# Two graph-attention layers on one core: the order of the last four turns and of a few opening steps is changed

## The chip, the cores and the metric

The kernel runs on one core of a Trainium2 chip. A core has a matrix engine (TensorE, PE in the profile; its weight loads are listed as PEld), VectorE (DVE), ScalarE (ACT), GpSimd (POOL) and SyncE (SP), which here issues all DMAs. Each engine works through its own queue of instructions in order; semaphores tie the engines together. TensorE writes its results to eight banks of PSUM, from which VectorE and ScalarE read them.

The metric is the device time of one execution in microseconds (us). Before the change the median of three runs is 2775.55 us (2774.35 to 2775.74).

## What is computed

Two layers of attention over 128 graphs of 128 nodes with 512 features, in float32. Cut to what matters:

```python
# layer 0: 4 heads of 64, mask adj;  layer 1: 8 heads of 64, mask adj or the diagonal
q, k, v = split_heads(h @ Wq), split_heads(h @ Wk), split_heads(h @ Wv)
sim  = einsum('bhid,bhjd->bhij', q, k) * 64 ** -0.5
attn = softmax(where(mask, sim, very_negative))
out  = merge_heads(einsum('bhij,bhjd->bhid', attn, v)) @ Wo + bo
x    = layernorm(x + out)      # after each of the two layers
# layer 0: h = x;  layer 1: h = layernorm(x) * gamma + beta, Wq, Wk, Wv from w_qkv
```

## The kernel before, in words

The 128 graphs are taken in 64 groups of two. The kernel is a pipeline written out by hand: the schedule is manual, so the order of the calls in the source is the order in which each engine gets its instructions. A turn `step(s)` works on five groups at once: the projections of layer 0 for group s, scores and softmax of layer 0 for group s-1, attention and output product of layer 0 for group s-2, the projections of layer 1 (`qk`, `v`) for group s-3, the scores and softmax of layer 1 for group s-4, and attention and output product of layer 1 for group s-5. `opening()` does the first groups and turns the weights of layer 1, `step(s)` runs for s = 2 to 63, and then `closing_a()` (turn 64), `closing_b(65)`, `closing_b(66)` and `last()` (turn 67) empty the pipeline. Each of these closings has its own order of calls.

Three parts of work come in every turn: part 0 is the softmax of layer 0 (both graphs), parts 1 and 2 are those of layer 1, one for each graph. For each part `masked` copies the scores under the mask into a cleared tile `sm` (VectorE), `maxima` takes the negative maxima (VectorE), `exps` takes the exponentials and their sums (ScalarE, four per half), `normalised` takes the reciprocal of the sums (VectorE) and multiplies (GpSimd), `blocks` transposes 32 by 32 blocks (VectorE) and writes them to DRAM, `probs_arrive` fetches them in transposed order into `pT`, and `attend` multiplies them with v (TensorE) and copies the result to `aT` (ScalarE). `blocks_direct` transposes on TensorE instead. `cleared` sets the next `sm` tiles (GpSimd).

The products with weights use a scheme of seven half-size products in place of eight (Winograd's form of Strassen's). They are numbered 1 to 7 and accumulate in three banks:

```python
    INTO = {1: ("a", True), 2: ("c", True), 6: ("a", False), 5: ("f", True), 7: ("a", False),
            4: ("a", False), 3: ("f", False)}
```

Bank a takes 1, then 6, 7 and 4 on top of it; bank f takes 5, then 3. Between two products of one bank the partial sum must be read out: a later product waits for that read. In `qk` and `v` ScalarE copies the partial sums of 1, 5 and 6 away (`tap`, tiles `ev` and `eqk`, L348), VectorE adds them to 2, 7 and 3, and ScalarE copies 4. In `out_product` VectorE adds each of the seven to the residual row block `r` (L502). The sums of inputs (`sums`, `out_sums`, L303) are made on GpSimd, and the sums of weights (`weight_sums`, `combine`, L186) once at the beginning, on VectorE and GpSimd; those of layer 1's q and k, second block, are made in turn 3, one subtraction at a time between other work.

`stats` takes mean and variance of the finished rows (VectorE), `roots` takes the reciprocal root (GpSimd, L699 to L714) and puts two things off into lists: `norms` (ScalarE normalises the rows, and for layer 1 a DMA writes them out) and, for layer 0, `ratios` (GpSimd). `flush()` issues what is in the first list, `flush(latest)` the second. `addend` scales the rows by the ratio (ScalarE, L679) and adds the bias (GpSimd, L680).

Tiles with one tag share one buffer: a new tile waits until the one before has been read. `AT[0, g]` (tile `aT` of layer 0) lies in tag `qo1`, and `SO[0, g]` (its sums) in `qo0`, the buffers of layer 1's q, which `qk` products 7 and 3 write.

`last()` ends with `out_plain`, the output product of the last group without the scheme, in banks a0 and f0, and `norm_plain`, its addition and norm.

Of the kernel before, what the change touches and what calls it, by code (L numbers as in the profile page):

```python
# [17 lines left out]
P = 128  # L18
D = 64
G = 2  # L20
# [7 lines left out]
def kernel(ctx: ExitStack, tc: tile.TileContext, x, adj, wq, wk, wv, wo, bo,  # L28
# [28 lines left out]
    def flush(what=later):  # L57
        while what:
            what.pop(0)()
# [110 lines left out]
    wsqk = const.tile([P, 3, KH, I1], F32, name="wsqk")  # L170
    wsv = const.tile([P, 3, KH, I1 // 2], F32, name="wsv")

    def weight_sums(w, ws, *blocks_, steps=range(4)):

        for c in blocks_:
            h0, h1 = (1, 0) if w is w1qk else (0, 1)
            b11, b12 = w[:, c, h0], w[:, c, h1]
            b21, b22 = w[:, KH + c, h0], w[:, KH + c, h1]
            combine(b11, b12, b21, b22, ws[:, 0, c], ws[:, 1, c], ws[:, 2, c],
                    eng=nc.gpsimd if w is w1qk and c == 0 else nc.vector, steps=steps)  # L180

    def combine(b11, b12, b21, b22, t2, t3, t4, eng=nc.vector, steps=range(4)):

        todo = ((b12, b12, b11), (t2, b22, b12), (t3, t2, b11), (t4, b21, t2))
        for o, a, b in (todo[i] for i in steps):
            eng.tensor_tensor(o, a, b, op=ALU.subtract)  # L186

    def weight_sums_0():
# [352 lines left out]
    def with_self(g):  # L541

        if 0 <= g < NG:
            nc.vector.tensor_tensor(M[g], M[g], eye[:, None, :].to_broadcast([P, G, N]), op=ALU.max)
# [91 lines left out]
    def attend(s, *parts):  # L636

        for part in parts or PARTS:
            l = min(part, 1)
            g = s - (2, 5)[l]  # L640
            if not 0 <= g < NG:
                continue
            K = (K0, K1)[l]
            if part != 2:
                AT[l, g] = one.tile([P, G, K, N], F32, tag=("qo1", "aT1")[l], name=f"aT{l}_{g}")
            pT = PT.pop((g, part))
            if part == 2:
                pm = mm_tile(f"av{part}_{g}")
            else:
                pm = ps_st.tile([P, 512], F32, tag="af"[part], name=f"av{part}_{g}")  # L650
            pm = pm.rearrange("p (k n) -> p k n", n=N)

            for b in range(G) if l == 0 else (part - 1,):
                for h in range(HEADS[l]):
                    i, kk = h % 2, h // 2
                    at = b * K0 + kk if l == 0 else kk
                    v = (qkv0[:, b, kk, 0 if g % 2 else 3, i * D:(i + 1) * D] if l == 0
                         else V[1, g][:, b, h * D:(h + 1) * D])
                    nc.tensor.matmul(pm[i * D:(i + 1) * D, at, :].rearrange("p (a r) -> p a r", r=32), v,  # L659
                                     pT[:, :, i * K1 + at, :], start=True, stop=True)  # L660
            if l == 0:
                nc.scalar.copy(AT[l, g].rearrange("p b k n -> p (b k) n"), pm)
            else:
                nc.scalar.copy(AT[l, g][:, part - 1], pm)  # L664

    def out_sums(l, g):
        if not 0 <= g < NG:
            return
        K = HEADS[l] // 2
        so = SO[l, g] = one.tile([P, 4, K // 2, N], F32, tag=("qo0", "xs0")[l], name=f"so{l}_{g}")  # L670
        halves_sums(so, AT[l, g].rearrange("p b (h c) n -> p b h c n", h=2))

    def addend(l, g):
# [96 lines left out]
    def v(g, *which):  # L770
        for i in which:
            product("v", g, i)

    def qk(g, *which):
        for i in which:
            product("qk", g, i)
# [43 lines left out]
    def step(s):  # L820
# [22 lines left out]
        out_product(0, s - 2, 1, 2, *(() if s == 2 else (5,)))  # L843
        maxima(s, 2)
        product_0(s, 2)
        normalised(s, 0)
        out_product(0, s - 2, *((5,) if s == 2 else ()), 6, 3)
        exps(s, 1, 0)
        stats(0, s - 2, 0)
        if s == 2:  # L850
            turn(0, s + 1)
            arrive(0, s + 1)
        if s == 3:
            weight_sums(w1qk, wsqk, 1, steps=(0,))
        product_0(s, 6)
        exps(s, 1, 1)
        out_product(0, s - 2, 7)
        (blocks_direct if s == 2 else blocks)(s, 0)
        if s == 3:
            weight_sums(w1qk, wsqk, 1, steps=(1,))  # L860
        product_0(s, 5)
        out_product(0, s - 2, 4)
        normalised(s, 1)
        finish(s - 3, 0)
        stats(0, s - 2, 1)
        if s == 3:
            weight_sums(w1qk, wsqk, 1, steps=(2,))
        exps(s, 2, 0)
        product_0(s, 7)
        finish(s - 3, 1)  # L870
# [1 line left out]
        blocks(s, 1)  # L872
        product_0(s, 3)
        if s == 3:
            weight_sums(w1qk, wsqk, 1, steps=(3,))
        if s > 2:
            turn(0, s + 1)
        product_0(s, 4)
# [41 lines left out]
        out_product(1, s - 5, 7, 3, 4)  # L920
        q_in_order(s - 3)
        addend(0, s - 1)
        v(s - 3, 7)
        stats(1, s - 5, 0)
        v(s - 3, 3)
        stats(1, s - 5, 1)
        v(s - 3, 4)
        if s > 2:
# [4 lines left out]
    def closing_a():  # L933

        s = NG
        made = scores(s, 1, 2)
        attend(s, 0)
        masked(made, s, 1, 2)
        out_sums(0, s - 2)
        finish(s - 3, 0)  # L940
        attend(s, 1, 2)
        made = scores(s, 0)
        maxima(s, 1)
        out_product(0, s - 2, 1, 2)
        masked(made, s, 0)
        finish(s - 3, 1)
        out_product(0, s - 2, 5, 6)
        maxima(s, 2)
        flush()
        load_rows(s - 1)  # L950
        exps(s, 1, 0)
        qk(s - 3, 1)
        out_product(0, s - 2, 7, 3, 4)
        qk(s - 3, 2)
        stats(0, s - 2, 0)
        stats(0, s - 2, 1)
        maxima(s, 0)
        exps(s, 1, 1)
        qk(s - 3, 6)
        addend(1, s - 5)  # L960
        out_sums(1, s - 5)
        exps(s, 2, 0)
        qk(s - 3, 5)
        normalised(s, 1)
        out_product(1, s - 5, 1, 2)
        flush()
        exps(s, 2, 1)
        qk(s - 3, 7)
        blocks(s, 1)
        out_product(1, s - 5, 5, 6)  # L970
        normalised(s, 2)
        flush(latest)
        exps(s, 0, 0)
        qk(s - 3, 3)
        blocks(s, 2)
        probs_arrive(s, 1, 2)
        out_product(1, s - 5, 7, 3)
        exps(s, 0, 1)
        normalised(s, 0)
        out_product(1, s - 5, 4)  # L980
        qk(s - 3, 4)
        cleared(s + 1, 1, 2)
        addend(0, s - 1)
        addend(1, s - 4)
        stats(1, s - 5, 0)
        stats(1, s - 5, 1)
        with_self(s - 2)

    def closing_b(s):

        only = s == NG + 1
        made = scores(s, 1, 2)
        masked(made, s, 1, 2)
        v(s - 4, 1, 2)
        maxima(s, 1)
        exps(s, 1, 0)
        v(s - 4, 6, 5)
        if only:
            blocks(s - 1, 0)
            probs_arrive(s - 1, 0)  # L1000
        maxima(s, 2)
        flush()
        v(s - 4, 7, 3, 4)
        exps(s, 1, 1)
        attend(s, 1, 2)
        out_sums(1, s - 5)
        finish_direct(s - 3)
        exps(s, 2, 0)
        out_product(1, s - 5, 1, 2)
        normalised(s, 1)  # L1010
        attend(s, 0)
        out_sums(0, s - 2)
        qk(s - 3, 1)
        out_product(1, s - 5, 5, 6)
        exps(s, 2, 1)
        qk(s - 3, 2)
        blocks(s, 1)
        out_product(1, s - 5, 7, 3)
        normalised(s, 2)
        qk(s - 3, 6)  # L1020
        out_product(1, s - 5, 4)
        out_product(0, s - 2, 1, 2)
        qk(s - 3, 5)
        blocks(s, 2)
        probs_arrive(s, 1, 2)
        out_product(0, s - 2, 5, 6)
        stats(1, s - 5, 0)
        stats(1, s - 5, 1)
        out_product(0, s - 2, 7, 3, 4)
        qk(s - 3, 7)  # L1030
        stats(0, s - 2, 0)
        stats(0, s - 2, 1)
        cleared(s + 1, 1, 2)
        flush()
        qk(s - 3, 3, 4)
        flush(latest)
        addend(1, s - 4)
        with_self(s - 2)

    def last():  # L1040

        s = NG + 3
        made = scores(s)
        masked(made, s, 1)
        maxima(s, 1)
        v(s - 4, 1)
        attend(s)
        exps(s, 1, 0)
        masked(made, s, 2)
        maxima(s, 2)  # L1050
        exps(s, 1, 1)
        out_product(1, s - 5, 1, 2)
        exps(s, 2, 0, 1)
        out_sums(1, s - 5)
        normalised(s, 1)
        v(s - 4, 2, 6)
        addend(1, s - 4)
        v(s - 4, 5)
        out_product(1, s - 5, 6, 5)
        whole_again()  # L1060
        normalised(s, 2)
        v(s - 4, 7)
        blocks_direct(s, 1)
        v(s - 4, 3)
        out_product(1, s - 5, 7, 3)
        stats(1, s - 5, 0)
        out_product(1, s - 5, 4)
        v(s - 4, 4)
        attend(s + 1, 1)
        stats(1, s - 5, 1)  # L1070
        blocks_direct(s, 2)
        flush()
        out_plain(NG - 1, 0, 0)
        attend(s + 1, 2)
        out_plain(NG - 1, 0, 1)
        norm_plain(NG - 1, 0)
        out_plain(NG - 1, 1, 0, 1)
        norm_plain(NG - 1, 1)

    opening()  # L1080
# [35 lines left out]
```

## Time and profile before

| | |
|---|---|
| median of three runs | 2775.55 us |
| the profiled execution's own time | 2776.21 us |
| its span, first to last instruction | 2774.4 us |
| TensorE matmuls busy | 2744.8 us, 99% of the span |
| TensorE weight loads busy | 2180.9 us |
| VectorE busy | 1945.2 us |
| ScalarE busy | 1526.4 us |
| GpSimd busy | 1748.5 us |
| DMA, mean over the span | 202 GB/s |
| mean granted TensorE clock | 0.998 |

The busy share of TensorE in 40 equal slices of the span is nine tenths or more in all but the first and the last two. Turn 2 begins at about 37 us of the span, turn 3 at 56.5, turn 4 at 93, turn 64 (`closing_a`) at 2628.5, turn 65 at 2663.8, turn 66 at 2703.4 and turn 67 (`last`) at 2737.1; the last matmul ends at 2767.9.

A row of a timeline gives the start, the duration of one merged group, engine, line, operation, output tile and input tile, and in brackets the idle time before it and the engine and line that ended it.

### The profile page before, as it was taken

To read this page: it belongs to the slowest core of one execution; us is meant where nothing else is said; L and a number is where in the kernel's file an instruction comes from. 1 tells how busy PE (TensorE), PEld (TensorE's weight loads), DVE (VectorE), ACT (ScalarE), POOL (GpSimd) and SP (SyncE) were. 2 spreads that over 40 slices of the span, in tenths; PEclk is the share of its full clock that TensorE was granted. 3 is DMA by queue.
4 is the path that set the end of the run, shared out by engine and by line. 5 is a ranking of instruction groups with operands and counts; after the bars stand their busy time and mean duration, and the time that the engine had idled before them with its cause. 6 is when DMAs were issued, how large, how long until landed. Compare 5 with 4: busy or idle time off the path is not lost.

```text
span 2774.4 us, 53786 instructions
## 1 busy us (share of the span) xinstructions
PE 2744.8 (99%) x18353; PEld 2180.9 (79%) x18353; DVE 1945.2 (70%) x3537; ACT 1526.4 (55%) x4869; POOL 1748.5 (63%) x2311
## 2 busy tenths in 40 slices
PE   8999999999999999999999999999999999999988
PEld 8978778778777787787787777877877877878777
DVE  5677677677677776776776776777767767767654
ACT  4456465465565564554655655645546556556454
POOL 5566666666666666666666666666666666666654
PEclk9999999999999999999999999999999999999999
DMA  5567877777777778778777777787787777777731
GB/s 170 154 197 206 223 209 210 216 209 215 211 209 221 207 208 222 208 208 220 210 212 214 208 220 209 210 220 208 206 223 208 210 215 209 217 210 210 190 107 54
DMA packets 473760, 561.42 MB, mean 202 GB/s; under 512 B 52104, under 2 KB 366992, under 8 KB 473488
## 3 DMA queue, kind: packets, MB, share of 16 engines
q1 hardware_dynamic: 473488, 557.99, 71.7%
q8 instruction: 147, 2.41, 0.4%
q14 instruction: 125, 1.02, 0.1%
HBM read 299.37 MB, written 258.47 MB: 201 GB/s over the span
## 4 chain that ended last, share of the span: by engine, by line
PE 96%; DVE 1%; ACT 1%; POOL 1%; issue 0%; DMA 0%; SPq 0%; POOLq 0%; ACTq 0%; DVEq 0%
PE qka L339 16%; PE a L460 13%; PE oa L498 12%; PE va L339 8%; PE qkf L339 8%; PE av L659 6%; PE f L460 6%; PE of L498 6%; PE qkc L339 4%; PE vf L339 4%; PE c L460 3%; PE oc L498 3%; PE sc L531 2%; PE sc L536 2%; PE vc L339 2%; PE sc_a L536 2%
## 5 line engine op out<-in xcount | busy, mean ns | idle before, releaser
L580 ACT ACTIVATE sm<-sm,nmax 128x128 f32<-128x128 f32 x1536 | 595.8, 395 | 9.3 <-DVE nmax L571 5.5
L589 POOL TENSOR_TENSOR sm<-sm,rec 128x1024 f32<-128x1024 f32 x192 | 364.1, 1896 | 274.9 <-DVE rec L588 274.9
L680 POOL TENSOR_TENSOR r<-r,bias 128x1024 f32<-128x1024 f32 x128 | 301.6, 2356 | 142.0 <-ACT r L679 142.0
L502 DVE TENSOR_TENSOR r<-oa,r 128x256 f32<-128x256 f32 x508 | 212.1, 417 | 173.5 <-PE oa L498 139.2
L580 ACT ACTIVATION_READ_ACCUMULATOR sm<-sm,nmax 128x1 f32 x1536 | 298.2, 194 | 0.0
L348 ACT COPY ev<-va 128x256 f32<-128x256 f32 x128 | 47.6, 372 | 433.7 <-PE va L339 433.7
L699 POOL TENSOR_SCALAR ve<-mv 128x2 f32<-128x2 f32 x191 | 41.6, 218 | 377.8 <-DVE mv L692 367.3
L607 DVE STREAM_TRANSPOSE turnedp<-sm 128x1024 f32<-128x1024 f32 x188 | 233.5, 1242 | 45.7 <-POOL sm L589 40.5
L303 POOL TENSOR_TENSOR xs<-xT 128x256 f32<-128x256 f32 x256 | 187.1, 731 | 112.4 <-ACT xT L257 91.6
L571 DVE TENSOR_REDUCE nmax<-sm 128x8 f32<-128x1024 f32 x192 | 226.2, 1204 | 0.1
L339 PE MATMUL qka<-wsqk,xs 128*128 128x512 f32 x472 | 221.8, 592 | 0.0
L339 PE MATMUL qkf<-w,xs 128*128 128x512 f32 x472 | 221.8, 592 | 0.0
L498 PE MATMUL oa<-wso,so 128*128 128x256 f32 x760 | 206.2, 380 | 3.3 <-DVE rec L588 2.4
L498 PE MATMUL of<-wo,so 128*128 128x256 f32 x760 | 206.7, 381 | 1.5 <-DVE r L502 1.4
L725 ACT ACTIVATE r<-r,shift,root 128x512 f32<-128x512 f32 x254 | 192.7, 807 | 10.6 <-POOL shift L714 10.6
L565 DVE COPY_PREDICATED sm<-m,sc 128x512 f32<-128x512 uint8 x256 | 172.9, 728 | 13.0 <-PE sc L531 3.1
L339 PEld LDWEIGHTS qkf<-w,xs 128*128 128x128 f32 x472 | 89.7, 190 | 112.9 <-issue 112.9
L339 PEld LDWEIGHTS qka<-wsqk,xs 128*128 128x128 f32 x472 | 89.7, 190 | 112.9 <-issue 98.8
L691 DVE BATCH_NORM_STATS2 st<-r 128x6 f32<-128x512 f32 x254 | 174.9, 689 | 2.3
L551 POOL MEMSET sm<- 128x1024 f32 x192 | 174.9, 952 | 0.0
L303 POOL TENSOR_TENSOR so<-aT 128x256 f32<-128x256 f32 (+1 forms) x254 | 150.5, 592 | 23.5 <-ACT aT L664 20.1
L498 PEld LDWEIGHTS of<-wo,so 128*128 128x128 f32 x760 | 143.7, 190 | 22.4 <-issue 2.5
(182 smaller groups left out, 6788.8 us busy)
## 6 DMA issues: line engine op xcount, KB each, us to landing
scrp<-turnedp SPq DMA_DIRECT2D x188, 512.0 KB, 3.2
pT<-scrp SPq DMA_DIRECT2D x252, 256.0 KB, 4.7
scr<-turned SPq DMA_DIRECT2D x123, 512.0 KB, 3.0
raw<-scr SPq DMA_DIRECT2D x492, 128.0 KB, 3.9
r<-in_x_dram SPq DMA_DIRECT2D x63, 512.0 KB, 3.7
out_dram<-r SPq DMA_DIRECT2D x63, 512.0 KB, 3.4
pT<-scrp SPq DMA_DIRECT2D x248, 128.0 KB, 4.1
x<-in_x_dram SPq DMA_DIRECT2D x61, 512.0 KB, 5.9
```

The source lines that it names most:

```text
L303: nc.gpsimd.tensor_tensor(o, a0, a1, op=op)
L339: nc.tensor.matmul(o, lhsT, rhs, start=first and m == 0, stop=m == len(todo) - 1, skip_group_check=True)
L460: nc.tensor.matmul(acc[:, at * P:(at + 1) * P], lhsT, rhs, start=first and n == 0, stop=n == len(todo) - 1, skip_group_check=True)
L498: nc.tensor.matmul(acc, left[:, c], right[:, c], start=first and c == 0, stop=c == hk - 1, skip_group_check=True)
L502: nc.vector.tensor_add(part, acc, part)
L551: nc.gpsimd.memset(sm, NEG1 if part else NEG0)
L571: nc.vector.tensor_reduce(NMAX[part], SM[part], AX.X, ALU.max, negate=True)
L580: nc.scalar.activation(sm[:, i, k, :], sm[:, i, k, :], AF.Exp, bias=nmax[:, i, k:k + 1], accum_out=total[:, i, k:k + 1])
L589: nc.gpsimd.tensor_tensor(SM[part], SM[part], rec[:, :, :, None].to_broadcast([P, 2, K1, N]), op=ALU.mult)
L607: nc.vector.transpose(t.rearrange("p q (h r) -> p q h r", r=32), SM.pop(part).rearrange("p i k (q r) -> p q (i k) r", r=32))
L680: nc.gpsimd.tensor_tensor(R[g], R[g], (bias0, bias1)[l][:, None, :].to_broadcast([P, G, E]), op=ALU.add)
L725: nc.scalar.activation(R[g][:, b], R[g][:, b], AF.Identity, bias=shift[:, b:b + 1], scale=root[:, b:b + 1])
```

## The change

It moves calls in turns 2 to 4 and in the four closings, and gives two tiles of the last group (63) other buffers. No arithmetic is added or removed.

- Turn 2: the output products 5 and 6 are called before `normalised(s, 0)`.
- Turn 3: the four subtractions of `weight_sums(w1qk, wsqk, 1)` stand together, behind `product_0` 3; the argument `steps` goes.
- Turns 3 and 4: product 3 of v stands before product 7.
- Group 63: `AT[0, 63]` in tag `x`, `SO[0, 63]` in tag `raw0`.
- `closing_a`: VectorE's transposes of parts 1 and 2 and the reciprocal of part 2 stand behind additions of the output product; `addend(1, 60)` before `addend(0, 63)`; part 0 is transposed and fetched at the end of this turn, not within the next.
- `closing_b`: v's copies of products 6 and 5 stand before all exponentials; part 1 is normalised and transposed before the attention's sums; exponentials of part 2 after the attention of part 0; output products of layer 0 lie between the products of qk; `norms` at the end stand behind the key copy (qk 4) and `addend`; in turn 66 `addend(1, 63)` is called too.
- `last`: the attention before v's other products, v's copies between the exponentials, `out_plain` in one piece per graph.

```diff
@@ step
         product_0(s, 2)
+        if s == 2:
+            out_product(0, s - 2, 5, 6)
         normalised(s, 0)
-        out_product(0, s - 2, *((5,) if s == 2 else ()), 6, 3)
+        out_product(0, s - 2, *(() if s == 2 else (6,)), 3)
...
-        if s == 3:
-            weight_sums(w1qk, wsqk, 1, steps=(0,))
...
-            weight_sums(w1qk, wsqk, 1, steps=(3,))
+            weight_sums(w1qk, wsqk, 1)
...
-        v(s - 3, 7)
+        v(s - 3, 3 if s < 5 else 7)
         stats(1, s - 5, 0)
-        v(s - 3, 3)
+        v(s - 3, 7 if s < 5 else 3)
@@ attend, out_sums
-tag=("qo1", "aT1")[l]
+tag=("qo1", "aT1", "x")[2 if (l, g) == (0, NG - 1) else l]
-tag=("qo0", "xs0")[l]
+tag=("qo0", "xs0", "raw0")[2 if (l, g) == (0, NG - 1) else l]
@@ closing_a
         qk(s - 3, 7)
+        out_product(1, s - 5, 5, 6)
         blocks(s, 1)
-        out_product(1, s - 5, 5, 6)
+        exps(s, 0, 0)
+        qk(s - 3, 3)
+        out_product(1, s - 5, 7, 3)
         normalised(s, 2)
         flush(latest)
-        exps(s, 0, 0)
-        qk(s - 3, 3)
+        exps(s, 0, 1)
+        out_product(1, s - 5, 4)
         blocks(s, 2)
         probs_arrive(s, 1, 2)
-        out_product(1, s - 5, 7, 3)
-        exps(s, 0, 1)
+        qk(s - 3, 4)
         normalised(s, 0)
-        out_product(1, s - 5, 4)
-        qk(s - 3, 4)
         cleared(s + 1, 1, 2)
+        addend(1, s - 4)
         addend(0, s - 1)
-        addend(1, s - 4)
         stats(1, s - 5, 0)
         stats(1, s - 5, 1)
         with_self(s - 2)
+        blocks(s, 0)
+        probs_arrive(s, 0)
@@ closing_b
         v(s - 4, 1, 2)
         maxima(s, 1)
+        v(s - 4, 6, 5)
         exps(s, 1, 0)
-        v(s - 4, 6, 5)
-        if only:
-            blocks(s - 1, 0)
-            probs_arrive(s - 1, 0)
         maxima(s, 2)
-        flush()
-        v(s - 4, 7, 3, 4)
+        v(s - 4, 7, 3)
         exps(s, 1, 1)
+        v(s - 4, 4)
+        normalised(s, 1)
         attend(s, 1, 2)
         out_sums(1, s - 5)
+        blocks(s, 1)
         finish_direct(s - 3)
-        exps(s, 2, 0)
         out_product(1, s - 5, 1, 2)
-        normalised(s, 1)
         attend(s, 0)
         out_sums(0, s - 2)
+        exps(s, 2, 0)
         qk(s - 3, 1)
+        flush()
...
-        blocks(s, 1)
         out_product(1, s - 5, 7, 3)
-        normalised(s, 2)
         qk(s - 3, 6)
         out_product(1, s - 5, 4)
-        out_product(0, s - 2, 1, 2)
+        normalised(s, 2)
         qk(s - 3, 5)
+        out_product(0, s - 2, 1, 2, 5)
         blocks(s, 2)
         probs_arrive(s, 1, 2)
-        out_product(0, s - 2, 5, 6)
+        qk(s - 3, 7)
+        out_product(0, s - 2, 6, 3)
         stats(1, s - 5, 0)
+        out_product(0, s - 2, 7)
         stats(1, s - 5, 1)
-        out_product(0, s - 2, 7, 3, 4)
-        qk(s - 3, 7)
+        qk(s - 3, 3)
+        out_product(0, s - 2, 4)
+        cleared(s + 1, 1, 2)
+        qk(s - 3, 4)
+        addend(1, s - 4)
+        if s == NG + 2:
+            addend(1, s - 3)
         stats(0, s - 2, 0)
         stats(0, s - 2, 1)
-        cleared(s + 1, 1, 2)
         flush()
-        qk(s - 3, 3, 4)
         flush(latest)
-        addend(1, s - 4)
@@ last
         v(s - 4, 1)
-        attend(s)
         exps(s, 1, 0)
         masked(made, s, 2)
+        attend(s)
+        out_sums(1, s - 5)
+        v(s - 4, 2, 6)
         maxima(s, 2)
+        v(s - 4, 5)
         exps(s, 1, 1)
         out_product(1, s - 5, 1, 2)
...
         out_product(1, s - 5, 4)
...
+        out_plain(NG - 1, 0, 0, 1)
         stats(1, s - 5, 1)
-        blocks_direct(s, 2)
         flush()
-        out_plain(NG - 1, 0, 0)
-        attend(s + 1, 2)
-        out_plain(NG - 1, 0, 1)
+        out_plain(NG - 1, 1, 0, 1)
         norm_plain(NG - 1, 0)
-        out_plain(NG - 1, 1, 0, 1)
         norm_plain(NG - 1, 1)
```

## What I predicted, and why

> **What bounds the kernel now.** I read first the table of busy time by stretch, then TensorE's waits in the closing, then the timelines of the engines that end them. The chain that ended last is 96% TensorE, and in the middle TensorE does not idle at all:
>
> ```profile
> 0.00:160.00 160.00, 151.40 (x1214) 135.85 (x1215) 100.68 (x179) 77.00 (x237) 87.58 (x119) 1.00 0.53 162
> 160.00:2600.00 2440.00, 2440.00 (x16060) 1915.62 (x16059) 1750.38 (x3173) 1369.18 (x4378) 1568.24 (x2072) 1.00 0.76 212
> 2600.00:2774.40 174.40, 153.37 (x1083) 129.41 (x1081) 94.11 (x186) 80.24 (x255) 92.62 (x120) 0.97 0.36 100
> ```
>
> (Stretch, length, busy us of TensorE matmul, weight load, VectorE, ScalarE, GpSimd, granted clock, DMA share, GB/s.) Matmuls are neither added nor removed, and from turn 5 to the last full turn no engine's order changes. So only idle time can move: 8.6 us in the opening, 21.0 us in the closing, 6.5 us of that after the last matmul. The waits in the closing are:
>
> ```profile
> PE va L339 <- ACT ev L348: 4.8, 3, 2.0
> PE oa L498 <- DVE r L502: 3.0, 5, 0.9
> PE oa L498 <- DVE rec L588: 2.4, 1, 2.4
> PE av L659 <- DMA pT<-scrp: 2.1, 1, 2.1
> PE sc L536 <- ACT kt L432: 1.5, 1, 1.5
> PE qka L339 <- ACT aT L662: 0.7, 1, 0.7
> ```
>
> One loss is in no list of waits. After the 2.38 us wait the clock was granted at half:
>
> ```profile
> 2654.00:2655.00 1.00, 0.00 (x0) 1.00 0.00 0
> 2657.00:2658.00 1.00, 1.00 (x3) 0.50 0.28 93
> 2662.00:2663.00 1.00, 1.00 (x7) 0.50 0.17 27
> 2664.00:2665.00 1.00, 1.00 (x20) 1.00 1.00 238
> ```
>
> Finer stretches put the half clock at 2656.44 to 2663.27. Product 3 (of), product 4 (oa) and qka then took 1.75, 2.07 and 3.13 us, against 1.03, 1.03 and 1.95 elsewhere: about 2.9 us lost.
>
> [...] the two drops, at 2656.44 and, after the last matmul, 2772.47, lie 116.03 us apart, 34 windows of 3.413 us. [...] 2.29 us of idle inside one window dropped it, 1.8 us (at 2711.0 to 2712.8) didn't; and a window with 0.88 us idle kept it at half. [...]
>
> **The opening** (one answer each). Turn 2: the reciprocal at 44.81 waited for exponentials with the addition of product 5 behind it, and product 3 waited 1.43 us. With the additions first product 3 waits about 0.3, but the normalisation still ends at 46.99, so the transposes after it wait some 0.5: gain 0.65. Turn 3: the weight sums (0.6 to 0.8 us each) between additions cost waits of 0.53 and 0.67; after the additions they are done by about 74.2, and product 6 of qk needs them at 75.6 or later: gain 1.2. Turns 3 and 4: product 3 of v between 6 and 7 hides the 0.46 us wait for a copy, but product 4 must then wait for the addition of product 7 (matmuls 1.03, addition 0.42, where product 3 had lain): 0. Sum 1.85.
>
> **The closing, replayed by hand** with the durations of before; times on its clock, the opening's gain kept apart.
>
> Closing a, turn 64. Products 5 and 6 of the output are added before the transpose of part 1, so product 7 starts at 2652.8, not 2655.3. The transpose still waits for GpSimd until 2653.3 (1.2 us), then the addition for qo (0.6); product 7 is added by 2655.45, and product 4, ready at 2654.6, starts at 2655.5. One wait of 0.9 replaces 2.38 and 0.88, and the half clock goes: the next scores start at 2658.35, not 2663.83. Gain 5.5.
>
> Turn 65, start. The normalisation of part 0 can't be earlier (2659.36 as before: its reciprocal stands behind part 2's transpose). Then come on VectorE the statistics, the moved transpose of part 0 (2661.3 to 2662.5), four masked copies (2.5), one addition (0.35), two maxima (1.13 each), and only then, at 2668.0, product 7 of v is added. The copies of partial sums are early now, so products 7 and 3 don't wait; product 4, ready at 2665.6, waits 2.4 until 2668.05. Before, it started at 2673.37. Gain 5.3: the 2.0 us wait for the copy became this one.
>
> Turn 65, rest. ScalarE copies aT before exponentials, but attention must end first: the 0.7 us stays. The waits of 0.52, 0.61 and 0.73 for additions of the two output products nearly go (about 0.3 left), since qk's products now lie between them, which the tags x and raw0 permit. The scores of turn 66 start at 2696.15, not 2703.42. Gain 7.25.
>
> Turn 66, start. These rows tell what stands in the way:
>
> ```profile
> 2704.00 1.52 ACT L725 ACTIVATE r<-r,shift,root 128x512 f32<-128x512 f32 x2 [3.73 <-POOL shift L714]
> 2705.42 0.56 ACT L432 COPY kt<-qka 128x512 f32<-128x512 f32 x1
> 2705.89 1.33 ACT L679 ACTIVATE r<-r,ratio 128x512 f32<-128x512 f32 x2
> ...
> 2702.41 0.19 POOL L699 TENSOR_SCALAR ve<-mv 128x2 f32<-128x2 f32 x1 [3.69 <-DVE mv L692]
> ...
> 2707.30 2.36 POOL L680 TENSOR_TENSOR r<-r,bias 128x1024 f32<-128x1024 f32 x1
> ```
>
> The key copy kt now leads on ScalarE, so the scores don't wait 1.46. But on GpSimd the bias addition of group 61 now stands before the roots of group 63, and on ScalarE the norm of 63 stands before v's copies. From the end of product 4 at 2696.25: kt and ratios 1.85, bias 2.4, roots 1.6, norm 1.4, copy 0.4: product 6 of v starts at 2703.9, though ready at 2700.1. A new wait of 3.75 takes what kt and the later 1.98 us copy wait give: gain 5.0 at product 6; 7.05 at product 7, which no longer waits.
>
> Turn 66, end, and last. Rows of before:
>
> ```profile
> 2728.38 0.18 DVE L588 RECIPROCAL rec<-total 128x8 f32<-128x8 f32 x1
> 2730.05 0.42 DVE L502 TENSOR_TENSOR r<-oa,r 128x256 f32<-128x256 f32 x1 [1.49 <-PE oa L498]
> 2730.57 1.25 DVE L607 STREAM_TRANSPOSE turnedp<-sm 128x1024 f32<-128x1024 f32 x1
> ...
> 2742.35 1.97 PE L659 MATMUL av<-pT,v 128*64 128x128 f32 x32 [2.15 <-DMA pT<-scrp]
> ```
>
> The reciprocal of part 2 moves behind that addition (to 2730.4), the normalisation (1.9), the transpose and the DMA with it: the probabilities land 2.0 later against TensorE, and the wait of 2.15 becomes 4.15. Gain 5.1 at the attention. Behind it v's copies no longer wait for 12 exponentials (0.85 saved), the transposes wait about 0.2, and the plain output product waits 0.6 for the addition of product 4, now directly before it (same bank); with fewer small starts 0.5 is gained. The end after the last matmul stays at 6.5.
>
> Sum with the clock at full: 1.85 + 5.1 + 0.5 = 7.45.
>
> **The clock.** Three waits are at least as long as the 2.38 that dropped it: 2.4 (turn 65), 3.75 (turn 66), 4.15 (last). A window at half loses 1.7 us. The price is between nothing (windows split the waits) and two windows each, 10.2 us, as before's one drop held. If the windows lie as in before, all three drop; TensorE is then busy in the next window, so I take one each, 4.9 us, as an estimate. Gain 7.45 - 4.9 = 2.55; allowing for the first, which hangs on 0.1 us, 3.
>
> The profiled execution took 2776.21 (span 2774.4); the runs' median is 2775.55. I take the gain from the median: 2772.5.
>
> **The rivals.**
> 1. The moves do what the first wait shows and the clock hardly drops: 2775.55 - 7.45 = 2768.1. For it: 3.4 us windows may split each wait. Against: waits of 3.75 and 4.15 leave little room for that.
> 2. Slower, by one mechanism: the half clock holds. In before it held a second window because of 0.88 us idle. If each of the three waits is followed by three such windows, 9 x 3.41 = 30.7 us at half cost 15.4: 2775.55 - 7.45 + 15.4 = 2783.5. It decides once half-clock time passes 26 us. Against: at half speed TensorE is slower than what feeds it, so small waits vanish and the windows are busy.
> 3. The moves in the opening and turn 64 give nothing, because other waits take their place (GpSimd's normalisations, above): then 5.5 + 1.85 shrink to the clock drop avoided, 2.9, and the rest cancels against the new drops: about 2775.5. Against: TensorE's order and the additions are free at that point.
>
> **How the numbers follow.** My forecast 0.59 (its own range 2770.0 to 2775.5), first rival 0.24, slower rival 0.11, third 0.06. The range of 2767.5 to 2777.0 takes in the first and third and leaves out the slower one and an edge. A change under 0.2%, 5.55 us (2770.0 to 2781.1), is about what this kernel's measurement can't tell from none. Faster: most of the first rival and 0.05 of mine, 0.26. Slower: 0.11. Same: 0.63.
>
> **What would show it.** Right: no 2.0 us waits of va for a copy in turn 65, instead va for VectorE (2.4); in turn 66 va for ScalarE's copy some 3.75; av for pT some 4; oa for rec gone; half clock after those. Wrong: turn 66's copy comes before the norm's end, pT lands within 2 us of need, or the half clock lasts through a turn.

## The result, and the profile after

The changed kernel took 2776.46 us (median of 14 runs, 2775.42 to 2779.12), the kernel before beside it 2775.55 us (14 runs, 2773.80 to 2778.06). The ratio is 1.0005, with a 95% interval from 0.9996 to 1.0013: no change that can be measured. The profiled execution of the changed kernel took 2775.48 us (span 2773.7), against 2776.21 (span 2774.4) before.

First the busy time by stretch of the changed kernel, in the columns of the prediction's first fence (stretch, length, busy us of TensorE matmul, weight load, VectorE, ScalarE, GpSimd, granted clock, DMA share, GB/s):

```profile
0.00:160.00 160.00, 153.11 (x1224) 137.23 (x1225) 104.32 (x182) 77.01 (x237) 90.47 (x123) 1.00 0.54 165
160.00:2600.00 2440.00, 2440.00 (x16067) 1915.71 (x16066) 1750.84 (x3176) 1371.73 (x4385) 1566.85 (x2071) 1.00 0.76 212
2600.00:2773.70 173.70, 152.71 (x1066) 129.70 (x1064) 92.63 (x181) 78.84 (x249) 91.42 (x120) 0.96 0.36 100
```

TensorE idles 6.9 us in the opening (160.00 - 153.11), 1.7 less than before. In the closing it idles 20.99 us, against 21.03 before: the whole new order of four turns has taken nothing off the idle time. The list of TensorE's waits in the closing of the changed kernel (engine, tile, line waited for, us in total, times, longest) says what became of it:

```profile
PE av L658 <- DMA pT<-scrp: 5.4, 2, 4.0
PE va L338 <- ACT ev L347: 3.9, 1, 3.9
PE va L338 <- DVE v L362: 2.3, 1, 2.3
PE oa L497 <- DVE r L501: 1.5, 3, 0.8
PE op L748 <- ACT aT L663: 0.8, 1, 0.8
PE qka L338 <- ACT aT L661: 0.7, 1, 0.7
```

Before, the six rows added up to 14.5 us in 12 waits, the longest 2.4. Now they add up to 14.6 us in 9 waits, the longest 4.0. The rows of 2.4 for `rec`, 1.5 for `kt` and 4.8 in three copies `ev` have gone; three long waits stand in their place. They are these, in TensorE's timeline of the changed kernel (start, duration, line, operation, tiles, and in brackets the idle time before and what ended it):

```profile
2653.39 1.13 PE L497 MATMUL oa<-wso,aT 128*128 128x256 f32 x4 [0.84 <-DVE r L501]
...
2665.94 1.13 PE L338 MATMUL va<-wsv,xT 128*128 128x256 f32 x4 [2.27 <-DVE v L362]
2668.49 3.63 PE L658 MATMUL av<-pT,v 128*64 128x128 f32 x32 [1.42 <-DMA pT<-scrp]
...
2705.13 1.20 PE L338 MATMUL va<-wsv,xs 128*128 128x256 f32 x4 [3.89 <-ACT ev L347]
...
2739.88 3.42 PE L658 MATMUL av<-pT,v 128*64 128x128 f32 x32 [3.96 <-DMA pT<-scrp]
...
2760.07 7.17 PE L748 MATMUL op<-wo,aT 128*128 128x256 f32 x32 [0.75 <-ACT aT L663]
```

The first drop of the clock follows two waits that lie close together, 2.27 and 1.42 us; the others follow one long wait each. At each of the three places the clock fell to half, as stretches of one microsecond of the same kernel show (the clock is the third number from the end):

```profile
2670.00:2671.00 1.00, 1.00 (x13) 1.00 (x12) 1.00 (x1) 0.50 (x1) 0.00 (x0) 0.50 0.50 137
2707.00:2708.00 1.00, 1.00 (x4) 0.81 (x3) 0.78 (x1) 0.00 (x0) 0.00 (x0) 0.50 0.00 0
2741.00:2742.00 1.00, 1.00 (x13) 1.00 (x11) 0.00 (x0) 0.36 (x1) 0.00 (x0) 0.50 0.00 0
```

Each of the three half clocks lasts 3.41 us (2668.51 to 2671.92, 2706.06 to 2709.47, 2740.19 to 2743.60), with TensorE busy through all of it, and they begin 37.55 and 34.13 us apart, 11 and 10 times 3.413. The half clock in turn 64 before lasted 6.83 us (2656.44 to 2663.27), twice 3.413. A window is here such a piece of 3.413 us. In the first and third, half speed is the reason why the attention of 32 matmuls took 3.63 and 3.42 us; the same group took 1.97 before.

Why the two longest waits are there is read on the engines that end them. In turn 66 it is ScalarE's timeline of the changed kernel, and for the bias GpSimd's:

```profile
2697.37 0.59 ACT L431 COPY kt<-qka 128x512 f32<-128x512 f32 x1 [8.37 <-PE qka L338]
2697.85 1.33 ACT L679 ACTIVATE r<-r,ratio 128x512 f32<-128x512 f32 x2
...
2703.30 1.52 ACT L725 ACTIVATE r<-r,shift,root 128x512 f32<-128x512 f32 x2 [2.71 <-POOL shift L714]
2704.73 0.35 ACT L347 COPY ev<-va 128x256 f32<-128x256 f32 x1
```

```profile
2699.27 2.36 POOL L680 TENSOR_TENSOR r<-r,bias 128x1024 f32<-128x1024 f32 x1 [0.84 <-ACT r L679]
```

`kt` leads, and the scores no longer wait for it. But the copy `ev` that frees bank a stands behind a norm, that norm behind roots on GpSimd, and those behind 2.36 us of bias. In the last turn it is the reciprocal, in VectorE's timeline of the changed kernel:

```profile
2725.76 0.42 DVE L501 TENSOR_TENSOR r<-oa,r 128x256 f32<-128x256 f32 x1 [2.23 <-PE oa L497]
2726.10 0.19 DVE L587 RECIPROCAL rec<-total 128x8 f32<-128x8 f32 x1
2728.31 1.25 DVE L606 STREAM_TRANSPOSE turnedp<-sm 128x1024 f32<-128x1024 f32 x1 [2.01 <-POOL sm L588]
```

The addition waits 2.23 us for TensorE with the reciprocal behind it; the normalisation, the transpose, the write and the fetch of the probabilities follow only then. The attention, itself earlier on TensorE, waits 3.96 us for them.

### The profile page after: what moved, and what is told of

Same layout as the page of the kernel before. It is cut to its first block, busy times and chain, and to the rows that moved or that the text cites. A ratio compares the mean times of both kernels' runs of the same rounds, so it can differ in the third digit from the quotient of the medians.

```text
span 2773.7 us, 53791 instructions
## 1 busy us (share of the span) xinstructions
PE 2745.8 (99%) x18353; PEld 2182.6 (79%) x18353; DVE 1947.8 (70%) x3537; ACT 1527.6 (55%) x4869; POOL 1748.7 (63%) x2311
## 4 chain that ended last, share of the span: by engine, by line
PE 94%; DMA 1%; POOL 1%; DVE 1%; issue 0%; ACT 0%; SPq 0%; POOLq 0%; DVEq 0%; ACTq 0%
PE qka L338 15%; PE a L459 12%; PE oa L497 12%; PE va L338 8%; PE qkf L338 8%; PE av L658 6%; PE f L459 6%; PE of L497 6%; PE vf L338 4%; PE qkc L338 4%; PE c L459 3%; PE oc L497 3%; PE sc L530 2%; PE sc L535 2%; PE vc L338 2%; PE sc_a L535 2%
```

## The experiments

Each kernel below starts from the changed kernel unless the text says that it starts from the kernel before. The kernel before ran beside each; its medians lay between 2775.84 and 2776.50 us, and ratios are to those. The changed kernel was not run again beside them: "below the changed kernel" means below its 2776.46, when the kernel before had 2775.55.

### Two of the long waits, one at a time

The scaling and bias of group 61 go from the end of turn 65 into turn 66, behind v's copies:

```diff
         v(s - 4, 6, 5)
+        if s == NG + 2:
+            addend(1, s - 5)
         exps(s, 1, 0)
...
-        addend(1, s - 4)
         if s == NG + 2:
+            addend(1, s - 4)
             addend(1, s - 3)
```

> The changed kernel, but the addend of group 61 (ScalarE's scaling and GpSimd's bias addition) goes from the end of turn 65 into turn 66, behind v's copies. New-waits theory (three new waits and the half clock behind each ate the gain): the roots and the norm of group 63 come 3.2 us earlier, product 6 of v waits some 0.7 in place of 3.89, and no half clock follows: 1.7 more, less some 0.5 for the later exponentials; about 4.5 us under the changed kernel, near 2772. Rival (the closing is bound by the softmax chain through VectorE, GpSimd and DMA, and TensorE's waits only show its slack): the wait comes back at the next attention, at most 1 us under the changed kernel, 2775.5 or more.

Measured: 2772.78 us (21 runs), ratio 0.9989 (0.9983 to 0.9996), 3.7 below the changed kernel. Two rows of this kernel's list of TensorE's waits:

```profile
PE av L658 <- DMA pT<-scrp: 6.3, 2, 4.5
...
PE va L338 <- ACT ev L347: 0.7, 1, 0.7
```

The wait of 3.89 is 0.7, and the clock stayed full in turn 66. The wait of the last turn took some back: 4.46 in place of 3.96, with two windows of half clock (2734.1 to 2740.9) in place of one.

In the second kernel the reciprocal of part 2 in turn 66 is called ahead of the addition of product 4 again, as in the kernel before (behind those of products 7 and 3, not ahead of them, as the expectation has it):

```diff
         out_product(1, s - 5, 7, 3)
+        if s == NG + 2:
+            normalised(s, 2)
         qk(s - 3, 6)
         out_product(1, s - 5, 4)
-        normalised(s, 2)
+        if s == NG + 1:
+            normalised(s, 2)
```

> The changed kernel, but in turn 66 the reciprocal of part 2 stands ahead of the additions of products 7, 3 and 4 again, as in the kernel before. New-waits theory: the last attention waits about 2.0 for the probabilities, not 3.96, and mostly no half clock follows: 3 to 3.7 us under the changed kernel, near 2773. Rival (the landing of the DMAs, not the reciprocal's place, sets the wait): the wait stays above 3.5 and the time at 2776 to 2777.

Measured: 2772.71 us (21 runs), ratio 0.9989 (0.9982 to 0.9995), 3.75 below the changed kernel. TensorE's timeline of this kernel at the last attention:

```profile
2739.09 1.97 PE L658 MATMUL av<-pT,v 128*64 128x128 f32 x32 [1.83 <-DMA pT<-scrp]
```

The wait is 2.1 shorter, and the attention takes 1.97 again: no half clock, 1.7 us more, 3.8 in all. The first kernel lost 3.2 us of one wait and got 0.5 back in the last one and 0.4 in turn 65 (1.8 in place of 1.42). Its clock was at half for three windows as before, but for 2.6 us of one of them TensorE was waiting anyway, so that half speed cost nothing there. Its profiled execution is 2.86 us shorter (2772.62). Both waits are thus shown to be on the path that sets the end.

### Is the clock a cause, or only seen beside the waits?

Idle matmuls, whose results nothing reads, are put into the three waits: 2 in turn 65, 3 in turn 66, 3 in the last.

```diff
+    def fill(n, name):
+        t = mm_tile(name)
+        for _ in range(n):
+            nc.tensor.matmul(t[:, :256], ident, wo1[:, 0, :256], start=True, stop=True, skip_group_check=True)
...
         v(s - 4, 1, 2)
+        if s == NG + 2:
+            fill(3, "fill66")
```

> The changed kernel with matmuls of no use put into the three long waits (2 x 0.86 us in turn 65, 3 x 0.86 in turn 66, 3 x 0.86 in the last), so that TensorE is busy there and no wait gets shorter at its end. Clock theory: the half clock goes, 1.7 us each, some 5 us under the changed kernel, near 2771.5, though more matmuls run. Rival (what is slow behind the waits is bound by other engines, the clock is no cause): no gain, 2776 to 2777.

Measured: 2776.20 us (13 runs), ratio 0.9999 (0.9991 to 1.0008). It tells nothing for or against, because the filling was too small. TensorE's timeline of this kernel in turn 66:

```profile
2701.74 1.46 PE L781 MATMUL fill<-wo,ident 128*128 128x256 f32 x6
2705.80 1.13 PE L338 MATMUL va<-wsv,xs 128*128 128x256 f32 x4 [2.60 <-ACT ev L347]
```

Three idle matmuls took 1.46 us, about half of what was reckoned, 2.60 us of waiting was left, and the clock still fell at all three places. So the next kernel has 5 and 3 of them in turn 65, before and behind product 4, and 8 each in turn 66 and the last.

> As the first filling, but with enough of it: a matmul of this shape took 0.43 us there, not 0.86, so the waits stayed 1.4 to 3.1 long and the clock still fell. Now 5 and 3 of them in turn 65 (2.2 and 1.3 us), 8 in turn 66 (3.4), 8 in the last (3.4). Clock theory: no half clock in the closing, 1.7 us saved at each of three places, 4 to 5 us under the changed kernel, near 2772, and runs that agree more closely than its 2775.4 to 2779.1. Rival (the clock is no cause): 2776 or more.

Measured: 2773.87 us (13 runs), ratio 0.9994 (0.9985 to 1.0002), 2.6 below the changed kernel's median. TensorE's timeline of this kernel at the same place, and at the last attention:

```profile
2700.55 3.62 PE L781 MATMUL fill<-wo,ident 128*128 128x256 f32 x16
2704.61 1.13 PE L338 MATMUL va<-wsv,xs 128*128 128x256 f32 x4 [0.45 <-ACT ev L347]
...
2739.39 2.62 PE L658 MATMUL av<-pT,v 128*64 128x128 f32 x32 [2.22 <-DMA pT<-scrp]
```

In its profile the half clock is gone in turns 65 and 66 and remains at the last attention, where the probabilities landed late in this execution and left 2.22 us unfilled: their fetch was issued 5.0 us after the transpose, against 3.3 in the changed kernel. From the scores of one turn to those of the next, turn 65 took 39.98 us (41.02 in the changed kernel) and turn 66 33.87 (35.54), with more matmuls in both. So the half clock itself cost time there, 1.0 and 1.7 us. What it costs the whole execution is not settled by this kernel: the interval just takes in no change, the late fetch took 1.7 us back, and the profiled execution is 0.5 us shorter (2774.99). Nor did the runs agree more closely, as was expected: they span 5.2 us, those of the changed kernel 3.7.

The same was tried on the kernel before: 5 idle matmuls in its 2.38 us wait in turn 64.

> The kernel before with five such matmuls (2.2 us) in the one wait of 2.38 of turn 64, behind which its clock fell for two windows. Clock theory with windows that lie by chance: none of that half clock, but the other waits near 2 us keep theirs; 0 to 2.9 us under before by the run, about 1.5 in the median. Rival (that wait itself costs the time): no gain.

Measured: 2777.54 us (13 runs), ratio 1.0005 (0.9997 to 1.0013): no gain. TensorE's timeline of this kernel:

```profile
2655.46 1.10 PE L498 MATMUL oa<-wso,so 128*128 128x256 f32 x4 [0.23 <-DVE rec L588]
...
2659.04 1.13 PE L498 MATMUL oa<-wso,aT 128*128 128x256 f32 x4 [1.61 <-DVE r L502]
...
2661.88 0.37 PE L536 MATMUL sc_a<-kt,qo 64*128 64x128 f32 x1
```

The half clock there is gone, but product 4 starts 3.58 us after product 7, just as in the kernel before at half clock (2655.32 to 2658.90): it waits 1.61 for VectorE in place of 0.88. So the half speed just ahead of this wait was hidden by it. Behind it the gain is there: from the start of product 7 to the next scores (the third row) it took 6.42 us, in the kernel before 8.51 (2655.32 to 2663.83), so this half clock cost 2.1. It was lost again further on. In this execution the waits of 2.01 in turn 65 and 2.43 before the last attention dropped the clock, which their like in the profile of the kernel before did not.

### Parts of the change alone

The kernel before, with only the edits of turn 2 (products 5 and 6 ahead of the normalisation) and turn 3 (the four subtractions together):

```diff
+        if s == 2:
+            out_product(0, s - 2, 5, 6)
         normalised(s, 0)
...
         if s == 3:
-            weight_sums(w1qk, wsqk, 1, steps=(3,))
+            weight_sums(w1qk, wsqk, 1)
```

> The kernel before with two parts of the change alone: in turn 2 output products 5 and 6 ahead of the normalisation, in turn 3 the four weight sums together; v's order and all closings as before. My sum: 1.85 us under before, and product 1 of qk in turn 64, at 2604.36 in before, some 1.9 to 2.1 earlier; the median near 2773.5. Rival (other waits take their place before the steady turns): less than 0.5.

Measured: 2774.61 us (13 runs) against 2776.50, ratio 0.9993 (0.9985 to 1.0002): 1.9 us, at the edge of what can be told. In the profile it took 54.06 us from the start of turn 2 to that of turn 4, against 56.11 before: 2.05 saved (0.63 of it in turn 2: 18.67 against 19.30). These edits are likely to be worth what they save, since TensorE was busy for all of the 2440.00 us in the middle, in the kernel before as in the changed one, with no wait there to take them back.

The kernel before, with only the new order of turn 64:

```diff
+        out_product(1, s - 5, 5, 6)
         blocks(s, 1)
-        out_product(1, s - 5, 5, 6)
+        exps(s, 0, 0)
+        qk(s - 3, 3)
+        out_product(1, s - 5, 7, 3)
         normalised(s, 2)
```

> The kernel before with turn 64 of the changed one alone (additions ahead of transposes, part 0 transposed at the end of that turn); turns 65 to 67 as before. Plain sum: the waits of 2.38 and 0.88 become one of 0.9 and the half clock goes, 5.5 us under before, 2770. Chain theory: the scores of turn 65 come 5.5 earlier but VectorE's maxima only 2.9, and v's copies still stand behind exponentials, so product 7 of v starts only about 3.0 earlier; 3 us under before, 2772.5, with a wait for that copy of some 4.5 and perhaps a half clock behind it.

Measured: 2777.44 us (13 runs) against 2776.50, ratio 1.0003 (0.9994 to 1.0011): neither figure came. TensorE's timeline of this kernel in turn 65, and a stretch behind it:

```profile
2669.77 2.07 PE L339 MATMUL va<-wsv,xs 128*128 128x256 f32 x4 [4.55 <-ACT ev L348]
```

```profile
2671.00:2672.00 1.00, 1.00 (x3) 0.78 (x3) 0.05 (x1) 0.96 (x2) 0.00 (x0) 0.50 1.07 361
```

TensorE comes earlier to v, and waits there 4.55 us for the copy behind the exponentials, where it waited 2.00 before. Product 7 starts 1.76 us earlier than before (2671.53), and in this execution turn 2 began 1.1 us later, so 2.9 of the gain were left. The two windows at half clock that follow (2667.7 to 2674.55) take most of that, and the clock fell once more, behind a wait of 2.04 before the last attention. Turn 64 alone shows no gain. In the changed kernel, which has the edits of turn 65 too, 5.33 us of it are still there at product 4 of v; those edits alone were not tried.

### The wait that the prediction left out

In turn 65 the attention waits 1.42 us for `pT`, right after product 4 of v has waited 2.27. Here the second `maxima` goes behind the additions of products 7 and 3, so that product 4 comes earlier:

```diff
         exps(s, 1, 0)
-        maxima(s, 2)
         v(s - 4, 7, 3)
+        maxima(s, 2)
```

(in turn 65 alone.)

> The changed kernel with one move in turn 65: the second maximum behind the additions of v's products 7 and 3. New-waits theory: product 4 of v waits about 1.15 us less (2.27 to 1.1), and the attention behind it, whose probabilities land when they did, 1.15 more (1.42 to 2.5): no gain from the wait; between 0 and 1.7 by the clock. Rival (each wait removed is a gain): 1.15 under the changed kernel, with the attention's wait at 1.4.

Measured: 2777.01 us (13 runs), ratio 1.0005 (0.9997 to 1.0013). TensorE's timeline of this kernel:

```profile
2665.27 1.13 PE L338 MATMUL va<-wsv,xT 128*128 128x256 f32 x4 [1.16 <-DVE v L362]
2669.12 3.51 PE L658 MATMUL av<-pT,v 128*64 128x128 f32 x32 [2.72 <-DMA pT<-scrp]
```

The first wait fell by 1.11, the second rose by 1.30: one stood behind the other. The landing of `pT` decides. The changed kernel's DMA queue shows when it is issued:

```profile
2652.46 5.12 SPq L610 DMA_DIRECT2D scrp<-turnedp  x2
2661.41 1.75 SPq L220 DMA_DIRECT2D pT<-scrp  x4
2663.20 0.52 SPq L610 DMA_DIRECT2D scrp<-turnedp  x1
```

The transpose of part 2 ended at 2657.03, its fetch began at 2661.41, and the attention began at 2668.49. The last write, that of part 0, lies beside the fetch. To see whether it slows it, part 0 is transposed and written in turn 65:

```diff
         with_self(s - 2)
-        blocks(s, 0)
-        probs_arrive(s, 0)
...
         exps(s, 1, 0)
+        if s == NG + 1:
+            blocks(s - 1, 0)
+            probs_arrive(s - 1, 0)
         maxima(s, 2)
```

> The changed kernel, but part 0 of turn 64 is transposed and written within turn 65, ahead of the second maximum, no longer at the end of turn 64 (its place among the other work is then nearly that of the kernel before). If the write of part 0, issued right behind the fetch of parts 1 and 2, delayed that fetch: it lands about 6 us after its issue, not 7.0, and the wait of the attention is about 1.0 less. If it didn't: it lands 7 us after issue, and the attention of turn 65 starts when it did. In both cases product 4 of v waits about as before the move (the transpose still lies in front of its addition), and the time stays within 1.5 us of the changed kernel's, 2775 to 2778.

Measured: 2777.33 us (13 runs), ratio 1.0004 (0.9996 to 1.0013). With the write of part 0 at 2666.45 the attention, at 2670.01, still began 7.1 us after the issue of the fetch at 2662.87. So that write is not what delays it. The fetch is issued 3.9 to 4.7 us after the transpose in the nine profiles with the new turn 64, and 3.3 us after it in turns 64 and 66 of the kernel before. In the changed kernel the list of the DMA queue's own waits names the landing of the write, 3.7 us, as what held the fetch; why that write landed later stays open.

### Everything that was found, together

Both moves of the first two kernels, and further: in turn 64 the reciprocal of part 2 ahead of the additions of products 7 and 3; in both turns 65 and 66 v's additions of 7 and 3 ahead of the second `maxima`; in turn 65 the finishing of rows (`finish_direct`) ahead of the attention; in the last turn v product 2 ahead of the attention, and output product 4 ahead of the attentions of group 63, so that the buffer of `aT` is free in time.

```diff
         qk(s - 3, 3)
-        out_product(1, s - 5, 7, 3)
         normalised(s, 2)
+        out_product(1, s - 5, 7, 3)
...
-        v(s - 4, 1)
+        v(s - 4, 1, 2)
...
         out_product(1, s - 5, 7, 3)
+        out_product(1, s - 5, 4)
         stats(1, s - 5, 0)
```

> The changed kernel with both of these moves (addend of 61, reciprocal of turn 66) and with: the reciprocal of part 2 ahead of products 7 and 3 in turn 64; the second maximum behind the additions of v's 7 and 3; the turned rows ahead of the attention in turn 65; v's product 2 ahead of the last attention; the output product 4 ahead of the last transposes. New-waits theory: 3.2 + 2.8 at the two long waits, about 2 of the 3.7 in turn 65, 0.75 at the end, 5 of half clock: some 13 us under the changed kernel, near 2763.5, and faster than both. Rival (softmax chain): 3 us at most, 2773 or more.

Measured: 2764.03 us (5 runs, 2763.29 to 2765.20), ratio 0.9956 (0.9944 to 0.9969): faster than both kernels, 12.4 us below the changed one. Its list of TensorE's waits in the closing, and its last stretch:

```profile
PE av L658 <- DMA pT<-scrp: 2.0, 2, 1.2
PE oa L497 <- DVE r L501: 1.6, 3, 0.9
PE av L658 <- DVE rec L587: 1.2, 1, 1.2
PE va L338 <- ACT ev L347: 0.7, 1, 0.7
PE qka L338 <- ACT aT L661: 0.7, 1, 0.7
PE va L338 <- DVE v L362: 0.4, 1, 0.4
```

```profile
2600.00:2761.70 161.70, 148.56 (x1073) 126.82 (x1071) 93.01 (x183) 79.05 (x251) 92.15 (x120) 0.99 0.38 108
```

No wait is longer than 1.25 us, and the clock stays full until 2759.7, near the end. Against the changed kernel the span is 12.0 us shorter: 7.85 of them are idle time of TensorE (20.99 - 13.14), 4.15 are busy time (152.71 - 148.56). The stretch from 2600 us takes in 0.8 us more of turn 63 here, since this execution came to turn 64 later (2627.24 against 2626.46), so from turn 64 on the busy time is 4.9 less. As the matmuls are the same, I read this as the clock: three windows at half, at 1.7 us (half of 3.41), would be 5.1. This kernel alone does not separate it from the waits. What each of the further moves brings was not tried alone.

## Why the prediction was right

It forecast 2772.5 us with the range from 2767.5 to 2777.0, and "within 0.2%" as the likeliest. Its time was 4 us too low; the measured time lies inside the range, 0.5 us below its upper end. For this the width of the range did more than the forecast: 2776.46 lies above the forecast's own range (2770.0 to 2775.5), nearest to the third rival's 2775.5, and the gain of 3 us (a ratio of 0.9989) lies outside the measured interval. That nothing measurable would come was right; the small gain was not. Its steps against the profile after (gain: how much earlier than before TensorE gets there, without the opening's gain; the measured opening gain is 2.1):

| step | predicted | measured |
|---|---|---|
| opening, turns 2 and 3 | 1.85, v's order 0 | 2.1, of it 0.24 before turn 2; v's order 0 |
| turn 64: wait before product 4, gain | 0.9, 5.5 | 0.84, 5.49 |
| turn 65: wait before v product 4, gain | 2.4, 5.3 | 2.27, 5.33 |
| turn 65: wait of the attention for `pT` | none in the sum | 1.42 |
| turn 65: `aT`, additions | 0.7, about 0.3 | 0.69, 0.41 |
| scores of turn 66, gain less one window | 7.25 - 1.7 = 5.55 | 4.06 |
| turn 66: wait for `ev` | 3.75 | 3.89 |
| last: wait for `pT` | 4.15 | 3.96 |
| last attention to end of matmuls, against before | 0.5 less, 1.6 more for the clock: 1.1 more | 27.36 against 25.56: 1.8 more |
| after the last matmul | 6.5 | 6.5 |
| half clock behind the three long waits | one window each | one window each |

What went right is the replay by hand. All three long waits were named with the engine that ends them, and their lengths are off by 0.13 to 0.19 us. The reason given in each case, that an instruction waits and what is behind it on its queue waits too, is what the rows of ScalarE, GpSimd and VectorE show (`ev` at 2704.73 right behind a norm that had waited 2.71 us, the reciprocal at 2726.10 behind an addition that had waited 2.23), and what the kernels that undo one of them confirm. The clock, the one term that could not be read off (one window for each wait was an estimate), came as taken in the profiled execution: three windows, none held for a second. That was luck in part. In the kernel that writes part 0 in turn 65, which has waits of the same kind at the same three places (3.00, 3.89 and 4.40), the clock stayed at half for a second window in turns 65 and 66; its profiled execution took 2779.41 at a mean clock of 0.996, and four of the changed kernel's 14 runs have that mean clock.

Three terms were wrong in size:

- **The fetch of turn 65.** The sum let the attention follow product 4 with no wait. The prediction names no time for this landing. From the end of the transpose of part 2 to the attention it took 11.5 us (2657.03 to 2668.49). In the last turn of the kernel before it took 10.5 (2731.82 to 2742.35); even that would have left a wait of 0.5, as TensorE was free at 2667.07. The term is 1.4 to 1.5 us of the shortfall, and making product 4 earlier brought none of it back.
- **The end.** A wait of 0.6 for VectorE's addition was expected before `out_plain`, because it uses the same bank. The wait is 0.75, but for `aT`: the copy of group 63's attention needs the buffer that product 4 of group 62 still read, and product 4 had moved behind that attention. ScalarE's timeline of the changed kernel has the copy waiting for that product:

```profile
2759.43 1.07 ACT L663 COPY aT<-av 128x512 f32<-128x512 f32 x2 [3.01 <-PE oa L497]
```

With product 4 called earlier, in the last experiment, no wait of `op` is left in the list. The length was right and the reason wrong, and the expected gain of 0.5 did not come: 0.7 us worse in all.
- **The price of a half clock.** The prediction put the drop in turn 64 at 2.9 us. The kernel before with idle matmuls there shows that its first part was hidden by product 4's wait: the next scores came 2.1 us earlier, not 2.9. The step's total of 5.5 was right all the same, since it was made from start times and not from this price.

In the profiled execution these leave 0.7 us of gain in the span, where 2.55 was summed: 1.5 for the fetch and 0.7 for the end are missing, 0.25 more came in the opening. The medians went the other way by 0.9 us, which is not clear of noise, for the profiled execution is among the shortest of the changed kernel. Its seven runs with a mean clock of 0.998 took 2775.42 to 2776.52, and the four with 0.996 took 2777.76 to 2779.12. The step from one execution's gain to the median is the fourth miss: it took the execution shown as typical of how many windows fall.

The rivals: the first (clock hardly drops, 2768.1) fell to the three stretches at 0.50. The slower one (half clock held for nine windows) did not come; in the profile each drop lasted one window, in which TensorE had no idle time (3.41 us busy of 3.41), in that of the kernel that writes part 0 in turn 65, two of the three lasted two. The third (opening and turn 64 give nothing) had the nearest number, but is wrong step by step, as the table shows. Its thought, that other waits take the place, holds for turn 64 taken alone, where 4.55 us for the copy took its gain.

## What to carry to other kernels

When calls are moved in a pipeline written out by hand, add up the waits of the bounding engine before and after: here 14.5 us in 12 waits became 14.6 in 9, and the kernel stood still. A statistic or reciprocal that others need over GpSimd and a DMA should not stand behind an addition that waits for TensorE, as the reciprocal here did behind one that waited 2.23 us. Such an addition can itself go later: with the reciprocal ahead of it again the wait of the last attention was 1.83 us in place of 3.96, and TensorE's three waits for such additions stayed at 1.5 in all. For the clock it matters how a sum of waits is divided: with everything together two waits of 1.2 us kept it, and in the changed kernel one of 3.96 lost it for a window, so shorten the longest first. Waits that lie close together counted together: 2.27 and 1.42 us, of which 2.26 fell into one window of 3.41, lost it in turn 65.

## What the runs showed of the hardware

Whether a wait of about 2 us dropped the clock differed from profile to profile of like kernels. In the kernel before the wait of 2.38 did, and 2.15 before the last attention did not; with only the opening edits the 2.38 did not, and the 1.98 of turn 66 did; with the new turn 64 alone 2.04 did. Waits of 3.87 us and more dropped it in every profile here. Within each profile all drops from 2600 us on lie whole windows of 3.413 us apart, within 0.02 us: 11, 10 and 9 in the changed kernel (2668.51, 2706.06, 2740.19 and, after the last matmul, 2770.91), 34 in the kernel before. Each half clock of the closings that ended within the span lasted 3.41 or 6.83 us, one window or two. Taken modulo 3.413 us from the start of the span, they fall at another place in each profile (1.1 in the kernel before, 3.0 in the changed one, 0.7 with the reciprocal moved back).

Why waits of one length differ shows when the closing of each of the twelve profiles is divided into such windows, laid through its drops. Then TensorE's idle time inside one window goes with the clock of the next, in these profiles. At full clock, every window with 1.95 us idle or more was followed by half clock, and none with 1.80 or less; of the two between, the one with 1.86 was and the one with 1.89 was not. At half clock, every window with 0.75 us idle or more was followed by another at half (0.75, 0.88, 1.37, 2.04 and 2.60 in four kernels), and every one with 0.38 or less by full clock. A wait of 2.38 us cut in two by the edge of a window (0.96 and 1.42 with only the opening edits) dropped nothing. Three windows of the kernel that writes part 0 in turn 65, from its turn 66 (columns as above; what TensorE is not busy of 3.41 us is idle):

```profile
2702.82:2706.23 3.41, 0.90 (x5) 0.44 (x3) 0.78 (x2) 0.69 (x2) 2.91 (x7) 1.00 0.44 160
2706.23:2709.65 3.42, 2.04 (x5) 1.68 (x6) 2.06 (x3) 1.33 (x3) 0.94 (x3) 0.50 0.00 0
2709.65:2713.06 3.41, 3.41 (x10) 2.69 (x9) 0.61 (x1) 1.95 (x9) 0.00 (x0) 0.50 0.00 0
```

The first has 2.51 us idle and the clock falls; the second has 1.37 idle and the clock stays at half. In the changed kernel the same wait of 3.89 us ended 0.9 us before the edge of a window, and the clock came back after one.

The same order of instructions thus differed by 1.7 us, what a window costs, or more from run to run: the changed kernel's runs at a mean clock of 0.998 have a median of 2775.87 us, those at 0.996 one of 2778.85. That bounds what a change of 2 us can show. The clock is not the only cause of spread: turn 2 began at 37.00 to 38.33 us in the twelve profiles, earliest in the changed kernel's, though the calls before it are the same in all.
